# Image statistics pieces and column weights moved to other slots of a hand-written order (two 5x5 convolution layers, one core)

## The chip, the core and the metric

The kernel runs on one core of one Trainium2 chip. The metric is the device time of one execution, in microseconds (us). The core's engines each work through their own list of instructions in the order in which the kernel issues them: PE (TensorE, matmuls), DVE (VectorE), ACT (ScalarE), POOL (GpSimd) and SP (SyncE, which here issues almost all DMA transfers). Semaphores make an instruction wait for what another engine or a transfer has to deliver.

## The reference

The input is x, 8 images of 32 channels and 252 x 252 pixels in float32, and two weights of 32 x 32 x 5 x 5. Two layers follow each other, each of the same form:

```python
x = x + conv5x5_reflect(_gn(x), weight)   # the reference convolves by FFT
def _gn(v, G=16, eps=1e-5):               # 16 groups of 2 channels, per image
    g = v.reshape(B_, G, C_ // G, H_, W_)
    m = jnp.mean(g, axis=(2, 3, 4), keepdims=True)
    s = jnp.var(g, axis=(2, 3, 4), keepdims=True)
    return ((g - m) / jnp.sqrt(s + eps)).reshape(v.shape)
```

So before layer 0 of an image can run, the mean and the variance of each channel group over the whole image must be known; before layer 1, those of layer 0's output.

## The kernel before, in words

**Tiling.** An image is split by parity of row and column into four planes, which with 32 channels fill the 128 partitions. Along the rows, an image makes 8 tiles of 16 such rows (`c` from 0 to 7). A tile of image `b` in layer `l` is written (b, l, c). Each is a convolution by row transforms: `transform` builds six sets of inputs, the points, on DVE (points 2 and 4 in tile t24, 1 and 3 in t13, 0 and 5 in t05), and `conv` does three matmul products for each of the six points on PE (each is two instructions in the trace), into PSUM. Points 2 and 4 go first (tiles m), then 1 and 3 (tiles pairs), then 0 and 5 (tiles sums or extra). ACT carries the product of point 2 into the pair tile of point 1 and that of 4 into the one of 3, ahead of the matmuls that add to them: `seed(0)`, L696, and `seed(1)`, L698. It also copies them out (`evacuate`, L704), and so does `first_pair` with the first pair (L711). DVE then forms the output rows: `difference` (L715), `inner` (L723 and L724) and `parts05` (L729 and L730). The outer rows come from the sums of points 0 and 5: on ACT (L739), or on DVE (L737) where the points 0 and 5 are done at once.

**By columns.** From tile (1, 0, 2) on, most layer 0 tiles do points 0 and 5 by a column scheme with weights of their own. These are tile wc, computed once per image from its scaled weights: `halve_middle` on ACT (L479) and `column_weights` on DVE, three operations (L484 to L486).

**Statistics of the input.** Each further image is also read a second time, flat, in 14 pieces of 128 x 1134. `load_piece` (L247) issues the transfer from SP into one of two buffers (tile st), and `piece_sums` does a sum (L228) and a sum of squares (L234) on ACT. The pieces of image b+1 lie in the slots of image b's layer 0.

**Weights.** A layer's transformed weights are fetched (L467), scaled on ACT by the inverse standard deviation, in three parts (`scale_points`, L506), and the residual is added on POOL (L474). The inverse standard deviation itself comes from a short chain of DVE, PE and ACT operations (`finish_stats`: L325 to L378).

**Order.** `order` lists the tiles; each has a slot on PE. Image 0's layer 0 takes slots 0 to 7. After them a layer 0 tile of the next image and a layer 1 tile of the image before alternate, with two exchanges; the slots that matter are 8: (1, 0, 0), 9: (1, 0, 1), 10: (0, 1, 0), 11: (0, 1, 1), 12: (1, 0, 2). Every piece of work is entered by `at(t, fn, ...)` with a due time t. The whole table is sorted by t at the end, and issued in that order; so t decides nothing but the order within each engine's list. `begin(i)` is the nominal start of slot i, summed from planned lengths. It gives 122.4, 132.6, 147.9, 168.3 and 178.5 for slots 8 to 12. These are due times; the profile's clock runs some 37 to 47 us ahead of them here. In the loop over slots, t0, t1 and t2 are begin(i), begin(i + 1) and begin(i + 2).

**What lies where the change is.** The due times on ACT in slot 9 are: scale_points of the first weights of (0, 1) and piece 0 of image 2 at 136.9; seed(1) at 137.7 with its copy at 137.8; the second scale_points at 137.9; halve_middle at 138.0; first_pair at 140.3; pieces 1 and 2 at 142.4; the third scale_points at 143.4; the border copies of tile (0, 0, 7) (`reflect`, L829 to L840) at 144.4; squares of (1, 0, 0) (L824) at 146.1; outer rows of (1, 0, 0) (L739, twice) at 147.95. Slot 10 follows: seed(0) at 150.5 and seed(1) at 153.0, each with its copy, first_pair at 155.6, reflect of (1, 0, 0) at 155.7, its squares at 157.6, piece 3 at 157.7, squares of (1, 0, 1) at 161.4, its outer rows at 168.35. On DVE the column weights are due at 140.8, ahead of point1 (L577) at 141.0. On SP the loads are due at 130.4 (pieces 0 and 1), 139.5 (2), 145.0 (3 and 4) and 160.3 (5); the next SP entry after these is the load of image tile (1, 4) at 172.3. Piece p + 2 can be loaded only when both sums over piece p are done, since it takes its buffer.

Of the kernel before, what the change touches and what calls it, by code (L numbers as in the profile page):

```python
# [53 lines left out]
def tile_conv_preact_x2(ctx: ExitStack, tc: tile.TileContext, x: bass.AP, w0: bass.AP, w1: bass.AP, out: bass.AP):  # L54
# [7 lines left out]
    NCH = 8  # L62
# [26 lines left out]
    def at(t: float, fn, *args, **kw):  # L89
        table.append((t, len(table), fn, args, kw))  # L90
# [67 lines left out]
    def once(b: int, c: int) -> bool:  # L158

        return c < (NCH - 1, 3)[b] if b < 2 else False  # L160

    def parts(b: int, c: int):

        if once(b, c):
            return ((0, 10), (10, 6)) if (b, c) == (0, 0) else ((0, 2), (2, 14))
        return ((0, ROWS),) + (((ROWS, 2),) if c == NCH - 1 else ())
# [214 lines left out]
    def finish_stats(b: int, l: int, *times):  # L381
        for t, fn in zip(times, (moments, group_mean, deviations, group_var, variance, inverse)):
            at(t, fn, b, l)
# [86 lines left out]
    def add_residual(eng, u, ks):  # L470
        for cp, rp in quads:
            to = (2 * (1 - cp) + (1 - rp)) * Q
            dst = u[quad(cp, rp), ks, 1 + cp, to : to + Q]
            eng.tensor_add(dst, dst, resid[quad(cp, rp), ks])  # L474
# [440 lines left out]
    for n in ((0, 1, 0), (B - 2, 1, NCH - 2)):  # L915
        i = order.index(n)
# [8 lines left out]
    def by_columns(b: int, l: int, c: int) -> bool:  # L925
        if l == 0:
            return c < NCH - 1 and (b > 1 or (b == 1 and c > 1))
        return c in (1, 3, 5) and b == B - 1
# [4 lines left out]
    def begin(i: int) -> float:  # L933

        return sum(10.2 + (own + [0.0])[j] + (late[j - 1] if j else 0.0) for j in range(i))


    t0 = -100.0
# [53 lines left out]
    for i, (b, l, c) in enumerate(order):  # L992
        t0, t1, t2 = (begin(i + j) for j in range(3))
        if i in at_once:
            conv(b, l, c, t0, t1, m05=(extra[:, 0], extra[:, 1]))
        elif i + 1 == len(order):

            conv(b, l, c, t0, t0 + 12.75, 0.0, 0, 2, m05=(extra[:, 0], extra[:, 1]))
            conv(b, l, c, t0 + 12.75, t0 + 20.4, 0.0, 2, 4, m05=(sums05[:, 0], sums05[:, 1]))
        elif i + 2 == len(order):  # L1000
            conv(b, l, c, t0, t1, t1 + 10.3, later=5.1)
        else:
            conv(b, l, c, t0, t1, t2, later=10.2 + own[i + 1])
        if i + 1 < len(order):
            transform(t0 + (6.3 if i == 0 else 2.9), t1 + 0.2, *order[i + 1], free=t0, now=(b, l, c))
            nb, nl, ncx = order[i + 1]
            k = inputs.index((nb, ncx)) + 2
            if nl == 0 and 2 < k < len(inputs):
                for part in parts(*inputs[k]):
                    at(t0 + (14.0 if nb == 0 and part[0] == ROWS else 4.0), load, *inputs[k], *part)  # L1010
                    at(t1 + 0.2, borders, *inputs[k], *part)
                    if once(*inputs[k]):
                        kb, kc = inputs[k]
                        t = 5.25 if part[0] == 0 and (kb, kc) != (1, 0) else 13.55 if kb else 8.5
                        at(t1 + t, even_columns, *inputs[k], *part)
        if c == 0 and any(by_columns(b, l, k) for k in range(NCH)):
            t = begin(i - 1) if l == 0 and b > 1 else t1 if l == 0 else t0
            at(t + 5.4, halve_middle, b, l)
            at(t + 8.2, column_weights, b, l)
        if b and l == 0 and c == 0:  # L1020
            at(t0 + 0.1, begin_sums, b, 1)

        if l == 0 and b + 1 < B:
            wide = 1 if b == 0 else 2
            if c == 0:
                for j in range(2):
                    at(begin(i - 1) + 1.0 if b > 1 else t0 + (8.0 if b else 1.0), load_piece, b + 1, j)
            if c < NPIECE // 2:
                for j in range(2):
                    p = 2 * c + j  # L1030
                    t = (t1 if wide == 2 and j else t0) + (8.6 + 2.5 * j if wide == 1 else 14.5 if (b, p) == (1, 0) else 9.8)
                    at(t, piece_sums, b + 1, p)
                    if p + 2 < NPIECE:
                        at(t + 2.6, load_piece, b + 1, p + 2)
            if c == 2:
                at(t0 + 14, fetch_weights, b + 1, 0)
            if c == NCH - 1:
                finish_stats(b + 1, 0, *(t0 + t for t in (1.55, 3.5, 3.6, 6.9 if b else 7.7, 7.8, 8.4)))
                for j, ks in enumerate(pairs):
                    at(t0 + (9.5, 10.4, 11.3)[j], scale_points, b + 1, 0, ks)  # L1040
                    at(t0 + (10.4, 12.3, 14)[j], lambda b=b, ks=ks: add_residual(G, scaled[b + 1, 0], ks))
        if l == 0 and c == NCH - 1:
            te = t0 + 15.3
            at(te + 0.1, fetch_weights, b, 1)
            finish_stats(b, 1, *(te + t for t in (3.0 if b < B - 1 else 4.4, 6.85, 6.86, 10.25 if b else 9.9, 12.82, 13.55)))
            for j, ks in enumerate(pairs):
                at(te + (14.5, 15.5, 21)[j], scale_points, b, 1, ks)
                at(te + (15.5, 17.5, 22)[j], lambda b=b, ks=ks: add_residual(G, scaled[b, 1], ks))
# [36 lines left out]
```

## Time and profile before

| what | us |
|---|---|
| median of 3 runs | 1935.1 (1933.72 to 1935.49) |
| the profiled execution's own time | 1933.69 |
| its span, first to last instruction | 1931.9 |
| PE busy | 1893.9 |
| DVE busy | 1719.6 |
| ACT busy | 1390.2 |
| POOL busy | 238.2 |
| DMA queue 1, share of 16 engines' time | 61.8% |

The profile is of one execution, which takes 1.8 us more than its span. A line of a timeline gives the start and the length in us, the engine, the line of the code, the operation, the tiles written and read, how many instructions are merged, and in brackets the idle time before it with what released it. A line of waits gives the engine and line that waited, what it waited for, the total, the number of times and the longest. An answer by stretches gives for each stretch its length, the busy time of PE, of the weight loads, DVE, ACT and POOL with the number of instructions in brackets, the clock that was granted to PE (1.00 is full), the share of DMA engines busy and GB/s.

### The profile page before, as it was taken

What the parts mean: (1) busy time and instruction counts of PE and PEld (TensorE: products, weight loads), DVE (VectorE), ACT (ScalarE), POOL (GpSimd) and SP (SyncE); (2) the same over time, 40 slices, a digit from 0 to 9 for tenths busy, and PEclk for the clock granted to TensorE, in tenths of its full rate; (3) what the DMA queues carried; (4) which work ended last, traced back from release to release, by engine and by line L of the source; (5) the groups of instructions that cost most, each with busy time, mean ns of one, the idle gap of its engine ahead of it and who ended that gap; (6) DMA issues with size and microseconds to landing.
All of it is one profiled execution on the core that took longest, in us unless ns stands there. A gap on an engine that the chain in (4) does not pass through costs nothing.

```text
span 1931.9 us, 19268 instructions
## 1 busy us (share of the span) xinstructions
PE 1893.9 (98%) x5054; PEld 942.2 (49%) x5054; DVE 1719.6 (89%) x2882; ACT 1390.2 (72%) x2661; POOL 238.2 (12%) x541
## 2 busy tenths in 40 slices
PE   6998999999999999999999999999999999999998
PEld 5444444544544444544544444544544444444445
DVE  7988799989988999989989899988989989988896
ACT  5886677777777877777777787776877765655574
POOL 4543000120001200012000210002000020000100
PEclk7998999999999999999999999999999999999999
DMA  9876465667766675756866757766766645641133
GB/s 272 206 166 163 100 153 142 139 152 172 167 141 152 143 168 141 170 134 142 189 134 138 176 127 174 148 141 159 159 154 157 141 99 117 129 91 46 41 80 90
DMA packets 220974, 276.09 MB, mean 143 GB/s; under 512 B 16448, under 2 KB 204224, under 8 KB 218688
## 3 DMA queue, kind: packets, MB, share of 16 engines
q1 hardware_dynamic: 220384, 272.09, 61.8%
q10 hardware_dynamic: 480, 2.77, 0.4%
q8 instruction: 40, 0.66, 0.2%
q14 instruction: 70, 0.57, 0.1%
HBM read 207.41 MB, written 67.39 MB: 142 GB/s over the span
## 4 chain that ended last, share of the span: by engine, by line
PE 94%; DMA 2%; DVE 2%; ACT 1%; issue 0%; SPq 0%; POOL 0%; ACTq 0%; DVEq 0%; POOLq 0%
PE pairs L653 33%; PE m L653 33%; PE sums L653 16%; PE extra L675 4%; PE sums L675 4%; PE extra L653 4%; DMA st<-in_x_dram 1%; DMA xs<-in_x_dram 0%; DVE v L544 0%; ACT junk L824 0%; DMA wraw<-in_L_conv_weight_dram 0%; DVE sd L715 0%; DVE bn L273 0%; DMA out_dram<-o 0%; DVE t L584 0%
## 5 line engine op out<-in xcount | busy, mean ns | idle before, releaser
L653 PE MATMUL pairs<-t,u 128*128 128x504 f32 (+2 forms) x1548 | 687.2, 586 | 7.5 <-ACT pairs L698 7.0
L653 PE MATMUL m<-t,u 128*128 128x508 f32 (+3 forms) x1560 | 677.9, 582 | 5.0 <-DVE var L364 3.0
L653 PEld LDWEIGHTS pairs<-t,u 128*128 128x128 f32 x1548 | 291.2, 189 | 340.3 <-issue 326.0
L653 PEld LDWEIGHTS m<-t,u 128*128 128x128 f32 x1560 | 294.3, 190 | 333.8 <-issue 315.4
L881 ACT COPY o<-y 64x508 f32<-64x508 f32 x496 | 326.6, 659 | 8.5
L653 PE MATMUL sums<-t,u 128*128 128x508 f32 (+3 forms) x732 | 314.4, 577 | 0.0
L739 ACT ACTIVATE y<-sums 128x508 f32<-128x508 f32 (+2 forms) x120 | 64.0, 584 | 222.9 <-PE sums L653 222.9
L584 DVE SCALAR_TENSOR_TENSOR t<-v 128x1024 f32<-128x1024 f32 (+1 forms) x128 | 157.4, 1230 | 61.3 <-PE sums L653 61.3
L715 DVE SCALAR_TENSOR_TENSOR sd<-sd,pairs 128x504 f32<-128x504 f32 (+2 forms) x258 | 166.7, 670 | 47.9 <-PE pairs L653 44.7
L653 PEld LDWEIGHTS sums<-t,u 128*128 128x128 f32 x732 | 137.3, 189 | 143.9 <-issue 136.7
L145 POOL COPY xs<-xs 64x32 f32<-64x32 f32 (+3 forms) x74 | 36.5, 494 | 1081.4 <-DMA xs<-in_x_dram 828.4
L824 ACT ACTIVATE junk<-y,negk 128x1008 bf16<-128x1008 f32 (+1 forms) x144 | 148.2, 1029 | 8.8 <-DVE y L724 5.7
L704 ACT COPY sd<-m 128x504 f32<-128x504 f32 (+2 forms) x258 | 149.7, 580 | 1.5
L711 ACT COPY sd<-pairs 128x504 f32<-128x504 f32 (+1 forms) x129 | 74.5, 577 | 85.8 <-PE pairs L653 81.4
L698 ACT COPY pairs<-m 128x504 f32<-128x504 f32 (+1 forms) x129 | 72.6, 563 | 83.3 <-PE m L653 68.7
L544 DVE TENSOR_TENSOR v<-xs 128x1792 f32<-128x1792 f32 (+1 forms) x65 | 130.1, 2002 | 1.9 <-issue 1.1
L544 DVE TENSOR_TENSOR v<-y 128x1806 f32<-128x1806 f32 x64 | 129.9, 2029 | 0.0
L234 ACT ACTIVATE st<-st,negk 128x1134 f32<-128x1134 f32 x98 | 121.7, 1242 | 3.2
L228 ACT ACTIVATE st<-st 128x1134 f32<-128x1134 f32 x98 | 112.1, 1143 | 6.5 <-DMA st<-in_x_dram 5.2
L474 POOL TENSOR_TENSOR u<-u,resid 32x64 f32<-32x64 f32 x180 | 83.9, 466 | 199.5 <-ACT u L506 188.7
L567 DVE TENSOR_TENSOR t<-u 128x512 f32<-128x512 f32 (+2 forms) x129 | 89.7, 695 | 17.2 <-PE m L653 4.1
L675 PE MATMUL extra<-sdiff,wc 128*128 128x252 f32 (+1 forms) x400 | 100.8, 373 | 0.1
(172 smaller groups left out, 2207.7 us busy)
## 6 DMA issues: line engine op xcount, KB each, us to landing
xs<-in_x_dram SPq DMA_DIRECT2D x176, 504.0 KB, 8.3
st<-in_x_dram SPq DMA_DIRECT2D x111, 567.0 KB, 4.3
out_dram<-o SPq DMA_DIRECT2D x488, 126.0 KB, 6.5
u<-ud SPq DMA_DIRECT2D x15, 1152.0 KB, 5.7
xs<-in_x_dram SPq DMA_DIRECT2D x30, 441.0 KB, 6.4
xs<-in_x_dram SPq DMA_DIRECT2D x28, 472.5 KB, 8.3
ud<-uraw ACTq DMA_DIRECT2D x2, 1152.0 KB, 4.8
xtail<-in_x_dram SPq DMA_DIRECT2D x64, 31.5 KB, 6.4
```

What stands on the lines that cost most here:

```text
L228: A.activation(junk, src, AF.Identity, accum_out=acc[:, 0, i : i + 1])
L234: A.activation(junk, src, AF.Square, bias=negk, accum_out=acc[:, 1, i : i + 1])
L474: eng.tensor_add(dst, dst, resid[quad(cp, rp), ks])
L544: V.tensor_sub(v[:, r0:r1], t[:, r0 + 2 : r1 + 2], t[:, r0:r1])
L567: V.tensor_sub(ts[b, l, c][0][:, 0, j0:j1], got["u"][:, 1, j0:j1], got["u"][:, 0, j0:j1])
L584: stt(t, got["vt"][:, :, 0:2], -4.0, got["vt"][:, :, 2:4], ALU.mult, ALU.add)
L653: T.matmul(dst, u[:, k, 2 - i, :], rhs[:, j0 + i0 : j0 + i1, i : i + wo], start=(i == 0 and not add), stop=(i == 2), skip_group_check=add,)
L675: T.matmul(dst[:, 0, use], w, rhs[:, use], start=(i == 2), stop=True, skip_group_check=(i != 2))
L704: A.copy(got["sd"][:, 1 + e], m24[e][:, 0:n])
L715: stt(d, d, -2.0, pairs13[e][:, 0:n], ALU.mult, ALU.add)
L824: A.activation(dst, src, AF.Square, bias=negk, accum_out=acc[:, 1, at_ : at_ + 1])
L881: copy(got["o", h][halves[s], 0:m, cp::2], got["y"][halves[cp], r : r + m, :])
```

## The change

Two due times change, in the loop over the slots. Column weights of image 1 (tile wc for layer 0) are entered from t2 = begin(10) in place of t1 = begin(9): halve_middle at 153.3 (138.0 before), column_weights at 156.1 (140.8 before). They are first read in slot 12, at due time 187.0. The first four statistics pieces of image 2 get due times of their own, from the starts of slots 9 and 10: 142.4, 145.0, 157.7 and 163.4, in place of 136.9, 142.4, 142.4 and 157.7. The load of piece p + 2 goes with piece p, 2.6 behind it: 145.0, 147.6, 160.3 and 166.0 for pieces 2 to 5. The first two loads, all other pieces and the other images stay where they are. No instruction is added or taken away.

```diff
         if c == 0 and any(by_columns(b, l, k) for k in range(NCH)):
-            t = begin(i - 1) if l == 0 and b > 1 else t1 if l == 0 else t0
+            t = begin(i - 1) if l == 0 and b > 1 else t2 if l == 0 else t0
             at(t + 5.4, halve_middle, b, l)
             at(t + 8.2, column_weights, b, l)
...
                 for j in range(2):
                     p = 2 * c + j
-                    t = (t1 if wide == 2 and j else t0) + (8.6 + 2.5 * j if wide == 1 else 14.5 if (b, p) == (1, 0) else 9.8)
+                    t = (t1 if wide == 2 and j else t0) + (8.6 + 2.5 * j if wide == 1 else 9.8)
+                    if b == 1 and p < 4:
+                        t = begin(NCH + (1, 1, 2, 2)[p]) + (9.8, 12.4, 9.8, 15.5)[p]
                     at(t, piece_sums, b + 1, p)
                     if p + 2 < NPIECE:
                         at(t + 2.6, load_piece, b + 1, p + 2)
```

## The prediction

> **What bounds the kernel now.** I read the page's engine table first, then its clock row, then the waits of PE (TensorE), then the timelines of PE, ACT (ScalarE) and DVE (VectorE) around the longest wait that lies in the part of the order that the diff touches, and last the chain of waits.
>
> ```profile
> PE 1893.9 (98%) x5054; PEld 942.2 (49%) x5054; DVE 1719.6 (89%) x2882; ACT 1390.2 (72%) x2661; POOL 238.2 (12%) x541
> PEclk7998999999999999999999999999999999999999
> ```
>
> PE is busy for 98% of the span, so time can only come out of its idle 38 us, or out of slices in which its clock was lowered: the first, and the fourth (145 to 193 us). PE's waits say where the idle time is (columns: engine, line, what it waited for, us in total, times, longest):
>
> ```profile
> PE m L963 <- DMA st<-in_x_dram: 15.1, 1, 15.1
> PE pairs L653 <- ACT pairs L698: 7.0, 1, 7.0
> PE m L653 <- DVE var L364: 3.0, 1, 3.0
> ```
>
> The first is the start-up, the third lies at 1784 us; the diff touches neither. The second is one wait of 7.0 us, for one copy on ACT: the seed of pair 3 (L698). PE's timeline around it, and two answers of busy time and clock by stretch:
>
> ```profile
> 174.95 2.70 PE L653 MATMUL pairs<-t,u 128*128 128x504 f32 x6
> 184.64 5.41 PE L653 MATMUL pairs<-t,u 128*128 128x504 f32 x6 [6.99 <-ACT pairs L698]
> 189.84 5.12 PE L653 MATMUL sums<-t,u 128*128 128x378 f32 x12
> ...
> 180.60:184.00 3.40, 0.00 (x0) 0.00 (x0) 0.51 (x2) 2.67 (x5) 1.83 (x6) 0.50 0.35 137
> 187.40:190.80 3.40, 3.40 (x6) 1.60 (x5) 1.78 (x4) 3.34 (x7) 0.66 (x1) 0.50 0.20 33
> ```
>
> The six matmuls ahead of the wait take 2.70 us, the same six after it 5.41: the granted clock is 0.50 (third figure from the end of a stretch) from about 180.6 to 190.8. Why the seed is late, on ACT:
>
> ```profile
> 177.77 0.94 ACT L506 ACTIVATE u<-u,rstd 128x768 f32<-128x768 f32 x1 [0.27 <-DVE rstd L378]
> 181.27 1.15 ACT L228 ACTIVATE st<-st 128x1134 f32<-128x1134 f32 x1 [2.56 <-DMA st<-in_x_dram]
> 182.78 1.24 ACT L234 ACTIVATE st<-st,negk 128x1134 f32<-128x1134 f32 x1
> 184.02 0.57 ACT L698 COPY pairs<-m 128x504 f32<-128x504 f32 x1
> 186.59 1.15 ACT L228 ACTIVATE st<-st 128x1134 f32<-128x1134 f32 x1
> ```
>
> Piece 0 of the third image (L228 and L234) stands ahead of the seed: ACT waits 2.56 us for its transfer, sums it for 2.75, and only then runs L698. DVE waits in the same place, for the halved weights (L479), which stand behind the seed on ACT:
>
> ```profile
> 186.26 0.42 DVE L485 SCALAR_TENSOR_TENSOR wc<-wc 128x256 f32<-128x256 f32 x1 [5.15 <-ACT wc L479]
> ```
>
> [...] half rate of 10.2 us, with edges at 180.6 and 190.8, outlasting the wait by 6.2. [...] L698's input was complete near 175 and it ran at 184.02, right after the piece.
>
> **The change, part by part.** Slots 8, 9, 10 and 11 are image 1's tiles 0 and 1 in layer 0, and image 0's tiles 0 and 1 in layer 1. In due times, piece 0 goes from 136.9 to 142.4, piece 1 from 142.4 to 145.0, piece 2 from 142.4 to 157.7, piece 3 from 157.7 to 163.4. The first two loads stay at 130.4, so piece 0 still lands at about 181.25 on the profile's clock: all up to 177.77 is unchanged.
>
> *ACT in slot 9, rebuilt.* A step is the time from one start to the next in the trace of before. L506 at 177.77 (step 0.83, from 185.00 to 185.83), seed L698 at 178.60 (0.51), L704 at 179.11 (0.47), L506 at 179.58 (0.83), L711 at 180.41 (0.46), piece 0 from 181.27 when its data is there (2.75, 181.27 to 184.02), the third L506 at 184.02 (0.83), the border copies of image 0's last tile at 184.85 (2.04, 192.43 to 194.47), piece 1 at 186.89 (2.52, 186.59 to 189.11), squares L824 at 189.41 (1.14), two L739 from 190.55 (1.03), slot 10's first seed L696 at 191.58, done 0.66 later at 192.24.
>
> *PE, rebuilt.* The seed ends at 178.60 + 0.57 = 179.17, and PE starts 0.05 later as it does now (184.59 to 184.64): 179.22 in place of 184.64, **5.4 us won**. A wait of 179.22 - 177.6 = 1.6 remains, behind two table steps and DVE's reciprocal standard deviation. Does 1.6 us idle lower the clock? At 1783.8 to 1786.8 PE idles for 3.0 us, and both stretches of 3.4 us around that show clock 1.00; at 33.8 to 37.2 two waits of 1.5 and 0.6 us with short matmuls were followed by 0.50. So the bounds are nothing and one 3.4 us spell at half rate, 1.7 us; I take nothing. At full clock, pair 3 takes 2.56 (half of twelve matmuls' 5.11), the outer sums of slot 8 take 4.44 (the same shapes from 48.05 to 52.49) and slot 10's first twelve 5.11, in place of 5.40, 4.92 and 5.11. That is 2.84 + 0.48 = **3.3 won** from the clock. PE would be at slot 10's pairs at 179.22 + 2.56 + 4.44 + 5.11 = 191.33. Their seed is there at 192.24 + 0.05 = 192.3: a **new wait of 1.0**, the price of piece 1 being ahead of that seed. The chain of waits has them now at:
>
> ```profile
> 200.07 5.11 PE pairs L653 x12
> ```
>
> The gain is 200.07 - 192.3 = **7.8 us** (5.4 + 3.3 - 1.0, rounded).
>
> *Pieces 2 and 3* cost ACT the same 2.5 us each, in slot 10. Now only piece 3 stands there, and ACT still idles 5.92 us ahead of L739 at 215.62. Rebuilt from 191.58 on: two copies and the second seed to 193.8, halved weights 0.3, L711 after pair 1 ends (192.3 + 2.56) to 195.4, border copies 1.34, squares 1.45, piece 2 2.52, squares 1.24, piece 3 2.52: 204.5. PE ends the sums that L739 reads at 192.3 + 5.11 + 5.11 + 0.12 + 5.18 = 207.8. So 3.3 us of cover are left and they cost nothing; without cover, each would be 2.5.
>
> *Loads of pieces 2 to 5* go behind their summing on SP (SyncE, the DMA queue): 2 and 3 wait for pieces 0 and 1 to free a buffer (184.0, 189.4), 4 and 5 for pieces 2 and 3 (about 200.7, 204.5). They pass no other SP entry: the next is the image tile load at due 172.3, which waits for DVE's L559 until 216.65 now (208.9 shifted). Transfer took 3.4 to 13.0 us from issue to landing, and pieces 2 and 4 are wanted 14 or more us after their issue. No cost. POOL's queue (GpSimd) keeps its order.
>
> *Column weights.* Their three DVE operations (0.43 + 0.42 + 0.42, some 1.2 us) and the 0.40 us L479 leave slot 9 and enter slot 10, where ACT has L479 done at 194.2, ahead of DVE at about 198. DVE's 5.15 us wait goes; behind it stood point 1 (L577) and the differences L715, which now wait for PE instead. In slot 10 the 1.2 us stand ahead of L577, L715 and L737; DVE had waits of 0.80 and 1.56 there and 4.14 in slot 11, and slot 11's points are done near 203 for matmuls at 208 and later. Hidden; uncovered it would be 1.2. Their first reader comes at due 187.0.
>
> *Sum.* Behind slot 11 everything moves forward together: from 216 us on PE waits for 3.5 us in all, so nothing else can absorb the gain. Profiled execution: 1933.7 (span 1931.9 and 1.8 around it) less 7.8 gives 1925.9. It lies 1.4 below the median of the runs, 1935.1; the same difference from that gives **1927.3**.
>
> **The rivals.** *A, half rate stays.* The waits of 1.6 and 1.0 us leave PE with the clock lowered for two spells of 3.4 us, 1.7 lost in each: gain 7.8 - 3.4 = 4.4, 1930.7. For it: the case at 33.8. Against: the 3.0 us wait at 1784. *B, slower: piece 1 blocks slot 10's seed.* It is now ahead of L739 and L696, and PE waits 1.0 us there already, so each us that its data comes after 186.9 is a us of PE. The gain is gone at 7.8 us late (194.7); with 13 late and the 3.3 of half clock back, it ends at 1927.3 + 13 + 3.3 = 1943.6. Longest landing now is 13.0 us from issue, for it: but ACT started piece 1 at 186.59 without a DMA wait in the trace of before, and its load isn't moved. *C, nothing.* PE comes 7.8 us early to a transfer that doesn't come early (image tile loads 8.3 us, DMA engines busy 0.5 to 0.7) and waits there: 1935.1. For it: the busy DMA. Against: those loads are released by DVE, which moves forward too, and POOL, their first reader, waits for 30 us without PE noticing.
>
> **How the numbers follow.** A difference of under 0.2% (3.9 us) can't be told from none. Forecast 0.72, with 1924.8 to 1929.6 as its own range: no new wait and the clock's full return give 8.7, and run spread 1.4; at the other end a shorter half-rate spell in the runs of before (one 3.4 us shorter costs 1.7 less) and another 0.6 us of wait. A 0.14, B 0.06, C 0.08. Faster holds the forecast and A, 0.86; same 0.08; slower 0.06. The range reaches to A.
>
> **What would show it.** Right: PE's wait on L698 at 1.6 or less, clock 1.00 through 180 to 191, a wait of about 1 us on L696 at 192, no DVE wait on L479, slot 11's matmuls 7.8 us earlier. Wrong: a wait of several us on L696 or L739, clock 0.50 after 180 us, or a new wait on a transfer further on.

## The result and the profile after

The changed kernel takes 1927.89 us in the median of 7 runs (1925.67 to 1929.26), the kernel before 1935.1 (7 runs, 1933.72 to 1935.75): the ratio is 0.9962, 95% interval 0.9951 to 0.9974. It is faster by 7.2 us, 0.4% (by the interval, between 5.0 and 9.5 us). The profiled execution took 1926.09 us, 7.6 less than the one before, with a span of 1924.3.

The page of the changed kernel answers the two rows shown of before:

```profile
PE 1891.5 (98%) x5054; PEld 942.6 (49%) x5054; DVE 1720.0 (89%) x2882; ACT 1390.0 (72%) x2661; POOL 238.9 (12%) x541
PEclk7999999999999999999999999999999999999999
```

The fourth slice of the clock row is 9 now. PE's busy time fell by 2.4 us with the same 5054 matmuls, since matmuls at half clock count as busy for longer (5.41 us for the six below, 2.80 now); the rest is idle time that went. Its waits and its timeline:

```profile
PE m L963 <- DMA st<-in_x_dram: 15.0, 1, 15.0
PE m L653 <- DVE var L364: 3.0, 1, 3.0
PE pairs L653 <- ACT pairs L698: 1.6, 1, 1.6
...
PE pairs L653 <- ACT pairs L696: 1.1, 2, 0.6
```

```profile
175.04 2.70 PE L653 MATMUL pairs<-t,u 128*128 128x504 f32 x6
179.33 2.80 PE L653 MATMUL pairs<-t,u 128*128 128x504 f32 x6 [1.60 <-ACT pairs L698]
181.97 4.60 PE L653 MATMUL sums<-t,u 128*128 128x378 f32 x12
186.41 5.27 PE L653 MATMUL m<-t,u 128*128 128x508 f32 x12
192.29 5.35 PE L653 MATMUL pairs<-t,u 128*128 128x508 f32 x12 [0.61 <-ACT pairs L696]
...
207.88 5.27 PE L653 MATMUL m<-t,u 128*128 128x508 f32 x12
```

The wait of 7.0 us has become one of 1.6 and one of 0.6. The six matmuls behind the first take 2.80 us where they took 5.41, and the answer by stretches has the clock (third figure from the end) at 1.00 where it was 0.50 before:

```profile
177.20:180.60 3.40, 1.80 (x5) 0.68 (x4) 3.19 (x10) 3.14 (x6) 0.62 (x2) 1.00 1.09 273
180.60:184.00 3.40, 3.40 (x11) 1.82 (x10) 3.36 (x7) 3.21 (x8) 2.94 (x8) 1.00 0.36 141
```

ACT's list shows the new order:

```profile
177.87 0.94 ACT L506 ACTIVATE u<-u,rstd 128x768 f32<-128x768 f32 x1 [0.26 <-DVE rstd L378]
178.71 0.57 ACT L698 COPY pairs<-m 128x504 f32<-128x504 f32 x1
...
181.22 1.15 ACT L228 ACTIVATE st<-st 128x1134 f32<-128x1134 f32 x1
...
191.50 0.65 ACT L696 ACTIVATE pairs<-m,means 128x508 f32<-128x508 f32 x1
```

The seed L698 stands directly behind the first weight scaling, and the piece behind it. From 181.22 to 192.1 ACT has no gap in which it waits: that is why slot 10's seed L696 is 0.6 us late.

The start-up differs between executions: in the ten traces slot 9's pair 1 starts anywhere from 174.29 to 175.86 us. So the experiments are also compared by the time from the start of slot 9's pair 1 to the first matmul of slot 11 in one trace, which covers all that the change touches on PE. The last column is the length of the matmuls above the 2.80 us (six behind a stop), 4.60 (sums) and 5.35 (twelve behind a stop) that they take in the changed kernel, at clock 1.00:

| kernel | median us | stretch, us | wait L698 | wait L696 | lost to half clock in this stretch, us |
|---|---|---|---|---|---|
| before | 1935.1 | 215.42 - 174.95 = 40.47 | 7.0 | none | 3.1 |
| changed | 1927.89 | 207.88 - 175.04 = 32.84 | 1.6 | 0.6 | none |
| e1, pieces only | 1928.77 | 208.67 - 175.74 = 32.93 | 1.6 | 0.7 | none |
| e2, weights only | 1935.08 | 215.15 - 175.86 = 39.29 | 6.9 | none | 2.0 |
| e3, piece 2 back | 1930.6 | 212.59 - 174.29 = 38.30 | 1.6 | 3.1 | 3.0 |
| e4, piece 1 later | 1926.86 | 206.95 - 174.94 = 32.01 | 1.6 | none | none |
| e5, variance early | 1925.56 | 208.34 - 175.63 = 32.71 | 1.6 | 0.5 | none |
| e6, seed first | 1928.86 | 210.61 - 175.39 = 35.22 | none | 3.3 | 1.6 |
| e7, loads early | 1931.68 | 211.69 - 175.54 = 36.15 | 4.3 | none | 1.4 |
| e8, together | 1923.8 | 205.77 - 174.62 = 31.15 | none | 0.8 | none |

### The profile page after: what moved, and what is told of

It reads as the page before. It is cut to its first block, busy times and chain, and to the rows that moved or that the text cites. A ratio compares the mean times of both kernels' runs of the same rounds, so it can differ in the third digit from the quotient of the medians.

```text
span 1924.3 us, 19269 instructions
## 1 busy us (share of the span) xinstructions
PE 1891.5 (98%) x5054; PEld 942.6 (49%) x5054; DVE 1720.0 (89%) x2882; ACT 1390.0 (72%) x2661; POOL 238.9 (12%) x541
## 4 chain that ended last, share of the span: by engine, by line
PE 94%; DMA 2%; DVE 2%; ACT 1%; issue 0%; SPq 0%; POOL 0%; ACTq 0%; DVEq 0%; POOLq 0%
PE pairs L653 33%; PE m L653 33%; PE sums L653 15%; PE extra L675 4%; PE sums L675 4%; PE extra L653 4%; DMA st<-in_x_dram 1%; ACT junk L824 0%; DMA xs<-in_x_dram 0%; DVE v L544 0%; DMA wraw<-in_L_conv_weight_dram 0%; DVE sd L715 0%; DVE bn L273 0%; ACT st L228 0%; DMA out_dram<-o 0%
## 5 line engine op out<-in xcount | busy, mean ns | idle before, releaser
L145 POOL COPY xs<-xs 64x32 f32<-64x32 f32 (+3 forms) x74 | 37.2, 503 | 1081.5 <-DMA xs<-in_x_dram 833.7
L698 ACT COPY pairs<-m 128x504 f32<-128x504 f32 (+1 forms) x129 | 72.6, 563 | 82.1 <-PE m L653 66.1
```

## The experiments

Theory: the whole gain is piece 0 leaving its place ahead of the seed, by the wait itself and by the half clock behind it; what limits it is ACT's work up to slot 10's first seed. Rivals: the column weights, at which DVE waited for 5.15 us, carry a part; or the piece's transfer alone was the trouble.

**e1, the pieces alone.** Against the changed kernel:

```diff
-            t = begin(i - 1) if l == 0 and b > 1 else t2 if l == 0 else t0
+            t = begin(i - 1) if l == 0 and b > 1 else t1 if l == 0 else t0
```

> The pieces moved as in the change, the column weights left at their old place. Theory (the whole gain is piece 0 leaving the place ahead of the seed of pair 3): as the changed kernel, within 0.3 us of span (1924.3), PE waits of 1.6 us on L698 and 0.6 to 0.9 on L696; DVE meets L479 already done, since that no longer stands behind a piece. Rival (DVE's 5.15 us wait for the halved weights held PE too): several us slower than the changed kernel, with DVE or PE waiting for L479 or L577.

The ratio to before is 0.9968 (0.9955 to 0.9980; the changed kernel's is 0.9962). The stretch is 32.93 us, 0.1 from the changed kernel's, with the same waits of PE, and DVE waits neither for L479 nor in place of it. The span itself was 1927.0, not within 0.3 of 1924.3: 0.7 us of that lie in the start-up, and 1.7 in half clock at 1780 us, told under e5. In slots 9 to 11 the theory holds.

**e2, the column weights alone.** Against the kernel before, the same line with t2. 

> The column weights moved alone, the pieces as in the kernel before. Theory: PE's wait on L698 stays at 7.0 us with half clock after it, and the span stays at 1931.9 within 0.5 us, though DVE's wait of 5.15 us on L479 is gone (DVE then waits for PE instead). Rival (that DVE wait carries part of the gain): 1 to 5 us faster than before.

Ratio 1.0002 (0.9994 to 1.0011): nothing. DVE's wait moved on to another result of ACT, which also stands behind the piece. The wait list of DVE for 165 to 216 us and PE's timeline:

```profile
DVE sd L715 <- ACT sd L711: 4.9, 1, 4.9
```

```profile
185.46 4.79 PE L653 MATMUL pairs<-t,u 128*128 128x504 f32 x6 [6.91 <-ACT pairs L698]
190.09 4.60 PE L653 MATMUL sums<-t,u 128*128 128x378 f32 x12
```

PE's wait stays at 6.91 us. The stretch is 1.2 shorter than before only because half clock cost 2.0 us in place of 3.1 in this execution (six matmuls took 4.79 us, not 5.41, and the sums were back at 4.60 from 5.12); the median shows none of it. So the change's second edit is worth nothing that these runs can show, by itself or on top of the first (e1).

**e7, the transfer.** Against the kernel before, the first two loads are issued ahead of an image tile's load:

```diff
-                    at(begin(i - 1) + 1.0 if b > 1 else t0 + (8.0 if b else 1.0), load_piece, b + 1, j)
+                    at(begin(i - 1) + 1.0 if b > 1 else t0 + (3.5 if b else 1.0), load_piece, b + 1, j)
```

> The kernel before with the loads of pieces 0 and 1 issued ahead of the load of image tile (1, 3) on SP (due time 125.9 in place of 130.4) and nothing else. It divides the old wait of 7.0 us into its transfer and its summing. Theory: piece 0 no longer waits for its transfer, so the seed comes 2.6 to 2.7 us earlier and PE's wait on L698 is 4.3; half clock stays for one or two spells. About 1932.4, 2.7 us faster than before. Rival (the transfer was all of it): wait near 1.6 and the time of the changed kernel; or (the tile load is now late) a new wait of POOL, ACT or PE.

Ratio 0.9986 (0.9980 to 0.9993), 2.9 us faster than before in the same session (1934.6). ACT and PE in its trace:

```profile
178.38 0.94 ACT L506 ACTIVATE u<-u,rstd 128x768 f32<-128x768 f32 x1 [0.27 <-DVE rstd L378]
179.22 1.13 ACT L228 ACTIVATE st<-st 128x1134 f32<-128x1134 f32 x1
...
181.96 0.57 ACT L698 COPY pairs<-m 128x504 f32<-128x504 f32 x1
...
182.58 4.21 PE L653 MATMUL pairs<-t,u 128*128 128x504 f32 x6 [4.34 <-ACT pairs L698]
```

The piece starts without a wait, the seed waits only for its summing, and PE for 4.3 us. So the old 7.0 us divide into 2.7 of transfer, 2.7 of summing and 1.6 for which the seed stands behind the first weight scaling. Half clock cost 1.4 us here (4.21 in place of 2.80).

**e3, how full slot 9 is on ACT.** Against the changed kernel, piece 2 goes back:

```diff
-                        t = begin(NCH + (1, 1, 2, 2)[p]) + (9.8, 12.4, 9.8, 15.5)[p]
+                        t = begin(NCH + (1, 1, 1, 2)[p]) + (9.8, 12.4, 12.5, 15.5)[p]
```

> The changed kernel with piece 2 back in slot 9, right behind piece 1 and ahead of the outer rows and of slot 10's first seed. Theory (ACT is full in slot 9, and each us put ahead of that seed is a us of PE): PE's wait on L696 grows from 0.6 by 2.5 to about 3.1 us, span 1926.8, clock 1.00 or one short spell at 0.50, then up to 1.7 more. Rival (ACT has room there, or the wait has another cause): span 1924.3, wait on L696 unchanged.

```profile
194.00 8.35 PE L653 MATMUL pairs<-t,u 128*128 128x508 f32 x12 [3.07 <-ACT pairs L696]
202.19 5.27 PE L653 MATMUL extra<-t,u 128*128 128x508 f32 x12
```

The wait is 3.07, as expected: what is put ahead of that seed is paid in full (2.46 us more wait for a piece of 2.5). The twelve matmuls behind it take 8.35 us in place of 5.35, with the clock at 0.50 from 194.0 to 197.4 and at 0.61 in the mean from there to 200.8: half clock costs 3.0, where I had allowed for 1.7. The median is 2.7 above the changed kernel's (1930.6, ratio to before 0.9978, 0.9971 to 0.9984). By the medians, more than a third of the 7.2 us thus hangs on piece 2 being in slot 10. In the profiled execution it is more, 5.5 of the 7.6 us of the stretch, but that one (1932.55) is among the slowest of the 19 runs.

**e4, one piece fewer.** Against the changed kernel, piece 1 goes behind slot 10's second seed:

```diff
-                        t = begin(NCH + (1, 1, 2, 2)[p]) + (9.8, 12.4, 9.8, 15.5)[p]
+                        t = begin(NCH + (1, 2, 2, 2)[p]) + (9.8, 5.3, 9.8, 15.5)[p]
```

> The changed kernel with piece 1 moved behind slot 10's second seed, so only piece 0 is left in slot 9. Theory: PE's wait of 0.6 us on L696 goes and nothing takes its place, since ACT's idle time of 3.4 us ahead of the outer rows in slot 10 takes the 2.5 us: span 1923.6. Rival (ACT is then too late for slot 11, or piece 3's load, which waits for piece 1, lands too late): a wait on L739 or on the seeds of slot 11, span 1924.3 or more.

```profile
186.32 5.27 PE L653 MATMUL m<-t,u 128*128 128x508 f32 x12
191.43 5.27 PE L653 MATMUL pairs<-t,u 128*128 128x508 f32 x12
```

PE's timeline has no wait between these two any more, and the stretch is 0.83 shorter, with no new wait in slot 10 or 11. The span is 1925.1, not 1923.6, again by half clock near 1780 (1.7 us); ratio 0.9960 (0.9948 to 0.9972).

**e6, the remaining 1.6 us.** Against the changed kernel, the seed goes first, and the first weight scaling and a border copy (L156) go behind it:

```diff
-                        t = 5.25 if part[0] == 0 and (kb, kc) != (1, 0) else 13.55 if kb else 8.5
+                        t = 5.25 if part[0] == 0 and (kb, kc) != (1, 0) else 15.65 if (kb, kc) == (1, 2) else 13.55 if kb else 8.5
...
-                at(te + (14.5, 15.5, 21)[j], scale_points, b, 1, ks)
+                at(te + (14.5 if b else 15.42, 15.5, 21)[j], scale_points, b, 1, ks)
```

> The changed kernel with the seed of pair 3 and its copy put ahead of the first weight scaling and of the border copy of image tile (1, 2) (L156), which goes behind the second scaling. Theory (ACT's work up to slot 10's first seed is the bound, not the first wait): PE's wait of 1.6 us on L698 goes, but the wait on L696 grows from 0.6 to about 2.6 us, since ACT ends that stretch some 0.4 later; slot 11 starts 0.3 to 0.5 us later than in the changed kernel counted from slot 9's pair 1. Rival (the waits are independent): the 1.6 us are won.

```profile
175.39 5.23 PE L653 MATMUL pairs<-t,u 128*128 128x504 f32 x12
180.46 4.60 PE L653 MATMUL sums<-t,u 128*128 128x378 f32 x12
184.90 5.27 PE L653 MATMUL m<-t,u 128*128 128x508 f32 x12
193.46 6.91 PE L653 MATMUL pairs<-t,u 128*128 128x508 f32 x12 [3.29 <-ACT pairs L696]
```

PE runs through pairs 1 and 3 without a stop, and loses all of it, and more, at the next seed. The direction is the theory's, the size is not: the wait is 3.29, not 2.6. Piece 0 starts 182.38 - 175.39 = 6.99 us after pair 1, against 181.22 - 175.04 = 6.18 in the changed kernel, so ACT came 0.8 later, not 0.4. ACT's list shows why:

```profile
178.22 1.76 ACT L506 ACTIVATE u<-u,rstd 128x768 f32<-128x768 f32 x2 [1.13 <-DVE rstd L378]
```

The first scaling cannot start before DVE has the reciprocal standard deviation. In the changed kernel the border copy of 1.83 us fills that time and ACT waits for 0.26 us; here it stands behind, and ACT waits for 1.13. And taking out the 1.60 us wait brought slot 10's first matmuls forward by (186.41 - 175.04) - (184.90 - 175.39) = 1.86. Half clock then took another 1.6 (6.91 in place of 5.35), so slot 11 starts 2.4 later than in the changed kernel, where 0.3 to 0.5 was expected. The ratio to before is 0.9968 (0.9955 to 0.9980). So the bound in slot 9 is ACT's list up to L696, its work and the idle time in it, and the wait on L698 was free as long as piece 1 stood there.

**e5, the spread of the runs.** The 3.0 us wait at about 1780 us is in both kernels. Against the changed kernel, one DVE operation of image 7's statistics is issued earlier:

```diff
-                finish_stats(b, 1, *(te + t for t in (3.0 if b < B - 1 else 4.4, 6.85, 6.86, 10.25 if b else 9.9, 12.82, 13.55)))
+                finish_stats(b, 1, *(te + t for t in (3.0 if b < B - 1 else 4.4, 6.85, 6.86, 10.25 if b else 9.9, 12.82 if b < B - 1 else 10.3, 13.55)))
```

> The changed kernel with one DVE operation of image 7's layer 1 statistics (L364) moved ahead of the differences L715, six operations earlier. It tests where the run to run spread of the changed kernel (1925.7 to 1929.3) comes from. Theory: the untouched 3.0 us wait of PE near the end is followed by 3.4 us at half clock in some runs and not in others (1.7 us); without that wait the median falls by 3 to 4.5 us against the changed kernel, to 1923.4 to 1925, and no half clock spell shows after 60 us. Rival (spread from start-up and transfers only): median 3.0 lower at most, same spread.

PE's waits on L364 and L698 in its trace:

```profile
1775.61 5.38 PE L653 MATMUL m<-t,u 128*128 128x508 f32 x12 [0.54 <-DVE var L364]
...
1784.66 2.82 PE L653 MATMUL pairs<-t,u 128*128 128x508 f32 x6 [1.12 <-ACT pairs L698]
```

The wait falls to 0.5, but the second seed behind it now waits 1.1 us, since it stands behind weight scalings for which the inverse standard deviation is still late. So only 1.3 us of the 3.0 are won there, and the median falls by 2.3 us, to 1925.56, less than expected (ratio to before 0.9954, 0.9940 to 0.9968, against the changed kernel's 0.9962 in another session: the two intervals overlap). The spread narrowed, from 3.6 us (7 runs) to 1.5 (5 runs). The same eight matmuls behind that wait, in the traces of the changed kernel and of e1:

```profile
1779.26 3.67 PE L653 MATMUL m<-t,u 128*128 128x508 f32 x8 [2.96 <-DVE var L364]
```

```profile
1780.06 5.37 PE L653 MATMUL m<-t,u 128*128 128x508 f32 x8 [2.96 <-DVE var L364]
```

So an equal wait of 2.96 us is followed by full clock in one and by half clock in the other, 1.7 us dearer. In the kernel before the eight took 3.67 too, in e3 and e4 5.26 and 5.33. For the other three traces with this wait, the time from slot 11's first matmul to the end of the span tells: 1718.2 us in e2 and 1718.0 in e7, as in e1, e3 and e4 (1718.2 to 1718.3), and 1716.6 in e6, as in the kernel before and the changed one (1716.5 and 1716.4). By that I count half clock in five of the eight. That explains why single spans of e1, e3 and e4 stand 1.7 us off; that it is also what spreads the runs of the changed kernel fits the narrower spread of e5, but with the start-up's own variation it isn't separated.

**e8, together.** The edits of e4, e5 and e6 on the changed kernel.

> The changed kernel with piece 1 behind slot 10's second seed, the seed of pair 3 first as in the run before the last, and L364 early. Theory: PE waits neither on L698 nor (more than 0.4 us) on L696 in slots 9 and 10, nor on L364: 1.6 + 0.4 + 3.0 = 5 us less than the changed kernel in one execution, 5 to 6 in the median, 1922 to 1923. Rival (slot 10's ACT work then runs into slot 11's seeds): a wait of 1 us or more there, 1924.

```profile
PE pairs L653 <- ACT pairs L696: 1.5, 3, 0.8
...
PE pairs L653 <- ACT pairs L698: 1.1, 1, 1.1
```

It is the fastest: 1923.8 us (1922.99 to 1924.18), ratio to before 0.9943 (0.9931 to 0.9956); all its runs lie below all of the changed kernel's. It misses the expected 1922 to 1923 by two waits: 0.8 on L696 in slot 10, since ACT is 0.8 later there as in e6 and PE is there 1.9 sooner, and the 1.1 on L698 of e5. With piece 1 gone from slot 9, the seed's move pays: 31.15 against e4's 32.01.

## Why the prediction was right

- *The wait on the seed.* Expected at 1.6 us: 1.60. Shown to be the piece by e1 and e7, and not the weights by e2.
- *The clock.* Taken as full after 1.6 us of idle time, and it was in all five traces that have this wait (the six matmuls behind it take 2.80 us in each). The trace of before shows a spell of the 3.4 us that it priced, from 37.3 to 40.7, at the first convolution (clock 0.51 from 37.2 to 40.6). The prediction had one case on each side and no number that decided between them, and the one it leaned on, the wait at 1784 us with full clock, shows half clock in five of eight traces. So this term came out right partly by luck. Pair 3 took 181.97 - 179.33 = 2.64 (2.56 expected), the sums 4.44 (4.44).
- *The new wait.* PE reached slot 10's pairs at 192.29 (192.3 expected), but the listed wait was 0.61, not 1.0, since PE itself came 0.35 later than 191.33: the seed of pair 3 ended 0.11 later, and the matmuls behind the one stop and ahead of the next took 0.24 more (2.64 in place of 2.56, 5.27 in place of 5.11). e6 says the same: a stop costs PE more than the wait that is listed, 1.86 for 1.60. That the start agrees to 0.01 is in part luck: the seed L696 ended at 192.15, 0.09 sooner than expected, and PE started 0.14 behind it, where 0.05 was expected.
- *The sum.* 7.8 expected, 7.6 by the profiled executions, 7.2 by the medians, whose interval can't tell these apart. The term that was off is the end point: I set the chain's 200.07 for an undisturbed block against the start of a block after a wait, which then takes 5.35 us in place of 5.11 (times of the chain). By the ends of the two blocks, it is 200.07 + 5.11 - 192.29 - 5.35 = 7.54. The forecast range's lower end does not quite follow from its own terms: 1935.1 - 8.7 - 1.4 is 1925.0, not 1924.8.
- *Pieces 2 and 3 in slot 10.* Expected to end at 204.5 with 3.3 us to spare: piece 3 ends at 204.7, and ACT then idles for 3.42 us. No cost, as e4 shows by adding a third piece there.
- *Loads.* No transfer wait came up. The tile load behind them was issued at 210.31, not at 208.9: it waits for DVE's L559, which ends at 210.25 and now has the column weights ahead of it (197.94 to 199.35). The prediction had priced these weights, but not for this load. PE didn't wait for it; POOL did, for 32 us where it had waited for 30.
- *Column weights.* DVE ran them at 197.94 to 199.35, with L479 done since 193.96; e1's stretch puts their place at 0.1 us.
- *Rival A* didn't come in slot 9, but its price, 1.7 us for one spell behind a wait, was right for the wait at 1780 us, and too low after 3.07 us, where half clock cost 3.0 (e3). *Rival B*'s rule, a us of PE for each us ahead of slot 10's seed, is what e3 measured (2.46 for 2.5); the piece's data was there in time. *Rival C* is out: the gain of 7.6 us at slot 11 is still there at the end.

## What to carry to other kernels

Where one engine feeds another in a fixed order, look at what stands ahead of the one instruction that the busiest engine waits for, and rebuild that engine's list step by step with measured starts, up to the next instruction of the same kind: the work that is moved back is due again there, and that second place decides how much is kept. A wait in a second engine at the same spot (here DVE's 5.15 us) can be a by-stander; moving its cause alone tells. Price a stop of PE as its listed wait, what the stop takes beyond that (here 1.86 us in all for 1.60 listed, e6) and half clock behind it (here 1.4 to 3.1 us after waits of 3.07 to 6.99, and nothing or 1.7 after 2.96).

## What was not expected of the hardware

After the idle time of 1.6 us in slot 9, PE ran at full clock in five of five traces (2.80 us for the six matmuls); after 2.96 us near 1780 half clock followed in five of eight; after 3.07, 3.29, 4.34, 6.91 and 6.99 us it followed each time, and cost 3.0, 1.6, 1.4, 2.0 and 3.1 us. The idle time alone doesn't decide, though. At the start of the first convolution, PE waits for 1.17 and 0.58 us in the changed kernel, ahead of and between matmuls of 128x252, and for 1.49 and 0.58 in the kernel before; there the clock was at half for 3.4 us in both, from 37.3 to 40.7. Nor does the work in the 3.4 us ahead decide by itself. Half clock followed 1.13 us of it in e3 (189.8 to 193.2), 1.62 in the kernel before and 1.65 in the changed one (both 33.8 to 37.2, the 128x252 matmuls). The clock stayed at 1.00 behind 1.80 us (177.2 to 180.6 in the changed kernel), but also behind 1.54 (1784.9 to 1788.3 in the kernel before) and 1.34 (1777.2 to 1780.6 in the changed one). What does decide was not found.

Two executions with the same wait of 3 us can therefore differ by 1.7 us (5.37 and 3.67 for the eight matmuls). The traces that show it are of different kernels with the same code at that place; each kernel has one trace.

A stretch in which PE was busy for 2.76 of 3.40 us (184.0 to 187.4 in the kernel before) was still followed by half clock (0.50 from 187.4 to 190.8, 0.99 from there on), and in e3 so was one with 2.60 us (193.2 to 196.6; the clock is 0.61 in the mean from 197.4 to 200.8). How long half clock lasts once PE works again differs. In the kernel before it is 6.2 us (184.6 to 190.8). For e2, e6 and e7 I estimate it as twice what half clock cost there, since six matmuls behind a stop take 5.41 us at 0.50 and 2.80 at 1.00: 4.0, 3.1 and 2.8 us. What sets this length these runs do not show.
